# Stacked graph layers on one core: self-loop blocks kept and restored by DMA instead of copies, GpSimd's share of the sums moved to VectorE, and a new rule for spacing the graphs in the planner

## The chip, the cores and the metric

The kernel runs on one NeuronCore of a Trainium2 chip. The metric is the device time of one execution in microseconds (us). Three runs of the kernel before took 2434.01 to 2434.8 us, with a median of 2434.67. The profiled execution, from which all durations below come, took 2439.81 us; its span from the first to the last profiled instruction is 2438.0 us.

## The reference, cut to what matters

There are 32 independent graphs. Each has a feature matrix x of 512 nodes by 256 features and a dense 512 by 512 adjacency matrix whose diagonal is never empty. Four layers follow each other, and each ends in a residual addition and a normalisation over the features. All data is float32.

```python
# layer 0
h = (1 + eps) * x + adj @ x
x = layernorm(x + relu(h @ W1 + b1) @ W2 + b2)            # 256 -> 512 -> 256
# layer 1
h = adj @ (x @ W.T + b)
x = layernorm(x + where(h > 0, h, alpha * h))
# layer 2
h = layer_norm(x, gamma, beta)
x = layernorm(x + (x + relu((adj @ h) @ W_rel + b_rel + h @ W_root)))
# layer 3
h = (eps * x + adj @ x) @ W1 + b1                         # 256 -> 1024
x = layernorm(x + silu(rmsnorm(h, w)) @ W2 + b2)          # 1024 -> 256
```

Layers 0 and 3 multiply by the adjacency with something added to its diagonal: (1 + eps) in layer 0 and eps in layer 3. Layers 1 and 2 use the adjacency as it is.

## The kernel before

**Products.** Most matrix products are done with seven block products instead of eight: `seven` (L552) calls seven products m1 to m7 and adds their results into the four quarters of the output. The price is sums of quarters beforehand: `left_sums` (L570) for the left factor and `right_sums` (L578) for the right one. `left_sums` of the adjacency gives s1 to s4 once per graph, and they serve all four layers. A result leaves PSUM either by a copy (`take`, ScalarE or VectorE) or by an addition on VectorE (`put`, an operand in PSUM).

**The adjacency of a graph** (`class Adjacency`, L599). Four DMA loads of 256 KB bring two halves. `sums` makes s1 to s4. Four pairs of 128 by 128 blocks hold the diagonal: one pair in each of the two loaded halves, one in s1 and one in s3, the last two in one tile (`with_diagonal`). They are copied to a spare tile (`kept`, three copies, one of them for s1 and s3 together, by GpSimd or ScalarE). `with_loops` (L636) writes block plus scaled identity over them, three additions, before layer 0's aggregation and again near the end of layer 2 for layer 3. `restore` (L632) copies the kept blocks back after layer 0's aggregation. `row_sums` (L643) adds up blocks for layer 1's bias.

**Engines.** TensorE does the products and transposes. VectorE does the additions from PSUM, the sums of quarters, and the statistics of the norms. ScalarE does activations, PSUM copies and most of the scaling of the norms. GpSimd takes powers for the inverse square roots (`inv_sqrt`, L484), the additions of a bias row (`plus_row`, L786), and some sums and copies. The queue of SP issues the loads of x and of the adjacency and the stores of the output.

**The order of the work is planned in Python.** Every operation is recorded with the engines that it may run on; where a call names `vector, gpsimd`, either may take it. `Plan.order` (L304) then lists all operations of all graphs: it keeps a clock per engine with the costs of L41 to L71, and at each step takes, among the operations that can start soonest, the one with the lowest rank. The rank of an operation of graph b is b times `period` plus the time at which the graph's own sequence of matmuls needs it, multiplied by `pace`; the last four graphs are set `last` apart instead of `period`. `near` weights operations that feed other engines. `best` (L298) tries every rule of `RULES` (L83) and keeps the order that its clock ends first; for the kernel before, this is period 84, pace 2, last 12, near 2. At most four graphs are in flight (`FLIGHT`, L424). They share 38 tiles of work space and the eight PSUM banks; the last tuple of a pool says how many tiles a graph must leave free, by its distance from the oldest graph in flight: `(0, 2, 2)` for the banks (L437).

The instructions are issued in that order, engine by engine, by one line (L252 for engine instructions, L268 for DMAs), so the profile shows these two lines for nearly everything, and groups are told apart by tiles and shapes. `room` is a work tile, `ps` a PSUM bank, `few` a small tile of statistics.

Of the kernel before, what the change touches and what calls it, by code (L numbers as in the profile page):

```python
# [10 lines left out]
AF = mybir.ActivationFunctionType  # L11
ALU = mybir.AluOpType

P = 128
# [5 lines left out]
def span(ap):  # L20

    n = 1
    for d in ap.shape[1:]:
        n *= d
    return n
# [37 lines left out]
def move_time(kbytes):  # L63
    return kbytes / 370, 2.8


def spread_time():
# [12 lines left out]

RULES = [  # L83
    (period, pace, 12, near)
    for period, pace in ((60, 1), (76, 1), (84, 2))
    for near in (0, 1, 2, 4)
]


class Pool:  # L90
# [91 lines left out]
class Plan:  # L182
# [81 lines left out]
    def move(self, engine, out, src, times, inward=True):  # L264


        def issue():
            getattr(self.nc, engine).dma_start(  # L268
                *(x.place() if isinstance(x, Part) else x for x in (out, src))
            )  # L270

        self.add({engine: (times, issue)}, out if inward else None, [] if inward else [src])

    def needs(self, pace, near):

# [22 lines left out]
    def best(self):  # L298


        rule = min(RULES, key=lambda rule: self.order(*rule)[0])
        return self.order(*rule)[1]
# [84 lines left out]
def tile_gnn_stack(ctx: ExitStack, tc: tile.TileContext, a: dict, out: bass.AP):  # L387
# [26 lines left out]
    B, N, D = a["x"].shape  # L414
# [6 lines left out]
    HC = NC // 2  # L421
    TH = N // 2
    FH = FC3 // 2
# [4 lines left out]
    psum = ctx.enter_context(tc.tile_pool(name="psum", bufs=1, space=bass.MemoryType.PSUM))  # L428
    plan = Plan(nc, FLIGHT)

    def pool(kind, name, n, size, grain, spare):
        return Pool(
            [kind.tile([P, size], F32, tag=f"{name}{i}", name=f"{name}{i}") for i in range(n)],
            grain, spare, kind is psum,
        )

    banks = pool(psum, "ps", 8, N, N, (0, 2, 2))  # L437
    rooms = pool(work, "room", ROOMS, NC * D, P, (0, 4, 6, 8))
    smalls = pool(work, "few", SMALL, 64, 4, (0, 2, 4))

# [1 line left out]
    def vector(method, n, *args, **kw):  # L442
        return "vector", method, vector_time(n), args, kw

    def gpsimd(method, n, *args, **kw):
        return "gpsimd", method, gpsimd_time(n), args, kw

    def scalar(func, n, x, **kw):
        return "scalar", "activation", scalar_time(n), (x,), dict(func=func, **kw)
# [18 lines left out]
    def add(o, x, y, *engines):  # L468
        both("tensor_add", o, x, y, engines or (vector,))

    def sub(o, x, y, *engines):
        both("tensor_sub", o, x, y, engines or (vector,))
# [7 lines left out]

    def stt(o, x, s, y, op0, op1):
        plan.do(o, vector("scalar_tensor_tensor", span(o), x, s, y, op0=op0, op1=op1))

    def inv_sqrt(o, x):  # L484
        n = span(o)
# [5 lines left out]
    def room(*shape):  # L491
        return Part(Room(rooms)).shaped(*shape)
# [76 lines left out]

    def left_sums(left, a21, s):  # L570

        sub(s[2], left["m1"], a21, vector, gpsimd)
        add(s[0], a21, left["m4"], vector, gpsimd)
        sub(s[1], s[0], left["m1"], vector, gpsimd)
        sub(s[3], left["m2"], s[1], vector, gpsimd)
        left.update(m5=s[0], m6=s[1], m7=s[2], m3=s[3])

    def right_sums(b11, b12, b21, b22, t):  # L578

        sub(t[0], b12, b11)  # L580
        sub(t[1], b22, t[0])
        sub(t[2], b22, b12, vector, gpsimd)
        sub(t[3], b21, t[1], vector, gpsimd)
        return dict(m1=b11, m2=b21, m3=b22, m4=t[3], m5=t[0], m6=t[1], m7=t[2])

    def weight_sums(name, a11, a12, a21, a22):
# [12 lines left out]
    class Adjacency:  # L599
# [15 lines left out]
        def sums(self):  # L615
            with_diagonal, others = room(HC, 2, TH), room(2, HC, TH)
            s1, s3 = (with_diagonal[:, :, i, :] for i in range(2))
            s2, s4 = (others[:, i] for i in range(2))
            left_sums(self.left, self.a21, (s1, s2, s3, s4))
            self.loops = [  # L620
                *(self.halves[j].strided(j * TH, (N + P, HC), (1, P)) for j in range(2)),
                with_diagonal.strided(0, (N + P, HC), (TH, 2), (1, P)),
            ]
            kept = room(4 * HC, P)
            self.plain = [
                kept[:, 0:HC], kept[:, HC : 2 * HC],
                kept[:, 2 * HC :].then(lambda v: v.rearrange("p (k s) n -> p k s n", s=2)),
            ]
            for d, o in zip(self.plain, self.loops):
                plan.do(d, gpsimd("tensor_copy", span(o), o), scalar(AF.Copy, span(o), o))  # L630

        def restore(self):  # L632
            for d, o in zip(self.plain, self.loops):
                plan.do(o, gpsimd("tensor_copy", span(o), d), scalar(AF.Copy, span(o), d))

        def with_loops(self, loop):  # L636
            for d, o in zip(self.plain, self.loops):
                wide = loop.unsqueeze(1)
                if len(o.shape) == 4:
                    wide = wide.unsqueeze(1)  # L640
                add(o, d, wide.to_broadcast(list(o.shape)), gpsimd, vector)

        def row_sums(self):  # L643

            rows = room(N)
            s1, a11, a12 = self.left["m5"], self.left["m1"], self.left["m2"]
            add(rows[:, TH:N], s1[:, 0, :], s1[:, 1, :], gpsimd, vector)
            add(rows[:, 0:TH], a11[:, 0, :], a11[:, 1, :], gpsimd, vector)
            for k in range(HC):
                add(rows[:, 0:TH], rows[:, 0:TH], a12[:, k, :], gpsimd, vector)  # L650
            return rows

    def aggregate(x, adjacency):
# [218 lines left out]
    def layer3(x, adjacency, b):  # L872

        aT = aggregate(x, adjacency)
        plus_row(x, b2_3)
        hT, acc = Wide(FC3), room(N)

        def squares(f):
            sq = room(2, N)
            act(sq, hT.pair(f), AF.Square)  # L880
            if f == 0:
                add(acc, sq[:, 0, :], sq[:, 1, :], vector, gpsimd)
            else:
                add(acc, acc, sq[:, 0, :], vector, gpsimd)
                add(acc, acc, sq[:, 1, :], vector, gpsimd)

        dense_feat(aT, A1_3, b1_3, hT, squares)
        few = small(2, NC)
        ve, rstd = few[:, 0, :], few[:, 1, :]
        column_sums(acc, lambda p, sums: ts(ve[p], sums, 1.0 / HID3, RMS_EPS, ALU.mult, ALU.add))  # L890
        inv_sqrt(rstd, ve)
        pr = bank(N)
        for c in range(NC):
            flip(pr[:, c * P : (c + 1) * P], rstd[:, c : c + 1].spread(P, P))
        t1, t2, t4 = (room(FH, TH) for _ in range(3))
        for q in range(0, FH, 2):
            for f in (q, q + 1, FH + q, FH + q + 1):
                mul(hT.chunk(f), hT.chunk(f), pr)
                act(hT.chunk(f), hT.chunk(f), AF.Silu, scale=w_3[:, f : f + 1])
            b11, b12 = (hT.pair(q)[:, :, j * TH : (j + 1) * TH] for j in range(2))  # L900
            b22 = hT.pair(FH + q)[:, :, TH:N]
            t1q, t2q = t1[:, q : q + 2], t2[:, q : q + 2]
            sub(t1q, b12, b11)
            sub(t2q, b22, t1q)
            sub(b12, b22, b12, vector, gpsimd)
            sub(t4[:, q : q + 2], hT.pair(FH + q)[:, :, 0:TH], t2q, vector, gpsimd)
        norm = Norm(x)

        def block(i, j):
            return x[:, j * HC : (j + 1) * HC, i * P : (i + 1) * P]  # L910

        def factor(m, k):
            if m in ("m4", "m5", "m6"):
                return dict(m4=t4, m5=t1, m6=t2)[m][:, k, :]
            f = k if m in ("m1", "m7") else FH + k
            j = 0 if m in ("m1", "m2") else 1
            return hT.chunk(f)[:, j * TH : (j + 1) * TH]

        def product(m, ps, first):
            for k in range(FH):  # L920
                for i in range(HC):
                    mm(
                        ps[:, i, :], factor(m, k)[:, i * P : (i + 1) * P], A2_3[m][:, k, :],
                        first and i == 0 and k == 0, k == FH - 1,
                    )

        def take(ps, i, j):
            add(block(i, j), ps, block(i, j))

        def put(ps, i, j, more):  # L930
            take(ps, i, j)
            if i == 1:
                norm.half(j)

        seven(*(bank(HC, P) for _ in range(3)), product, take, put)
        norm.scales((1.0, LN_EPS))
        y = norm.scaled()
        place = out[b].rearrange("(p c) d -> p c d", c=NC)
        plan.move("sync", place, y, move_time(N * D / 256), inward=False)
# [3 lines left out]
    x = load_x(0)  # L943
# [15 lines left out]
    x = layer0(x, adjacency)  # L959
# [23 lines left out]
    for b in range(1, B):  # L983
        plan.graph = b
        x, adjacency = load_x(b), Adjacency(b)
# [43 lines left out]
```

## Time and profile before

| | |
|---|---|
| device time, median of 3 | 2434.67 us |
| span of the profiled execution | 2438.0 us |
| TensorE clock granted | 0.997 |
| TensorE matmuls | 12808 |
| VectorE busy | 2050.2 us in 5249 instructions |
| ScalarE busy | 1226.0 us in 2490 instructions |
| GpSimd busy | 622.6 us in 677 instructions |
| DMA | 73.89 MB, mean 30 GB/s |

The profile's rows name the line, the engine (PE is TensorE, PEld its weight loads, DVE VectorE, ACT ScalarE, POOL GpSimd, SPq the queue of SP), the operation, and the tiles as output<-inputs. A group's row gives the count, the busy time, the mean of one in ns, and then the idle time of the engine just before its members with what ended it. A row of waits reads: who waited, for whom, total us, how often, the longest. A row of the chain or the timeline begins with the start and the length in us. A float32 matrix product stands in the trace as two matmuls for each one that the kernel writes, except transposes, so 12808 in the trace are 6596 written ones.

### The profile page before, as it was taken

To read this page: it belongs to the slowest core of one execution; us is meant where nothing else is said; L and a number is where in the kernel's file an instruction comes from. 1 tells how busy PE (TensorE), PEld (TensorE's weight loads), DVE (VectorE), ACT (ScalarE), POOL (GpSimd) and SP (SyncE) were. 2 spreads that over 40 slices of the span, in tenths; PEclk is the share of its full clock that TensorE was granted. 3 is DMA by queue.
4 is the path that set the end of the run, shared out by engine and by line. 5 is a ranking of instruction groups with operands and counts; after the bars stand their busy time and mean duration, and the time that the engine had idled before them with its cause. 6 is when DMAs were issued, how large, how long until landed. Compare 5 with 4: busy or idle time off the path is not lost.

```text
span 2438.0 us, 35804 instructions
## 1 busy us (share of the span) xinstructions
PE 2387.9 (98%) x12808; PEld 2117.5 (87%) x12808; DVE 2050.2 (84%) x5249; ACT 1226.0 (50%) x2490; POOL 622.6 (26%) x677
## 2 busy tenths in 40 slices
PE   7999999999999999999999999999999999999998
PEld 6888888888888888888888888888888888888888
DVE  7888888788888889888898788988888888888788
ACT  3454545545455454554554544545445455454464
POOL 2232222222222212232122232223222222222220
PEclk9999999999999999999999999999999999999999
DMA  5011001110011110111101111011110011101000
GB/s 177 1 35 35 10 26 35 36 35 10 27 35 35 35 35 1 35 35 35 35 1 35 35 35 36 1 35 35 35 35 9 28 35 36 35 1 35 1 1 35
DMA packets 34915, 73.89 MB, mean 30 GB/s; under 512 B 6832, under 2 KB 9648, under 8 KB 34736
## 3 DMA queue, kind: packets, MB, share of 16 engines
q1 hardware_dynamic: 30576, 71.05, 8.7%
q8 instruction: 101, 1.65, 0.3%
q10 hardware_dynamic: 4160, 0.54, 0.1%
q14 instruction: 78, 0.64, 0.1%
HBM read 54.80 MB, written 16.78 MB: 29 GB/s over the span
## 4 chain that ended last, share of the span: by engine, by line
PE 71%; DVE 23%; ACT 2%; DMA 2%; issue 1%; SPq 0%; POOL 0%; POOLq 0%; ACTq 0%; DVEq 0%
PE ps L252 71%; DVE room L252 19%; DVE few L252 4%; ACT room L252 2%; DMA room<-in_adj_dram 1%; DMA L_gnn_b<-in_L_gnn_b_dram 0%; SPq L268 0%; DMA room<-in_x_dram 0%; POOL few L252 0%; POOL room L252 0%; ACT L252 0%; POOLq L1025 0%; DVEq L252 0%; ACTq L1025 0%; ACTq L252 0%
## 5 line engine op out<-in xcount | busy, mean ns | idle before, releaser
L252 PE MATMUL ps<-room,room 128*128 128x256 f32 x3584 | 872.5, 382 | 20.7 <-DMA room<-in_x_dram 9.9
L252 PEld LDWEIGHTS ps<-room,room 128*128 128x128 f32 x3584 | 672.5, 191 | 122.3 <-DVE room L252 14.5
L252 DVE TENSOR_TENSOR room<-ps,room 128x256 f32<-128x256 f32 (+1 forms) x1024 | 523.7, 522 | 232.8 <-PE ps L252 194.6
L252 PE MATMUL ps<-L_gnn_W,room 128*128 128x128 f32 (+1 forms) x3584 | 623.0, 322 | 5.3 <-ACT room L252 3.4
L252 ACT ACTIVATE room<-room 128x1024 f32<-128x1024 f32 (+2 forms) x421 | 324.3, 773 | 564.2 <-DVE room L252 293.9
L252 PEld LDWEIGHTS ps<-L_gnn_W,room 128*128 128x128 f32 x3584 | 538.4, 191 | 58.1 <-ACT room L252 8.6
L252 DVE TENSOR_TENSOR room<-room,room 128x512 f32<-128x512 f32 (+1 forms) x825 | 491.4, 603 | 17.1 <-DMA room<-in_adj_dram 7.4
L252 POOL TENSOR_TENSOR few<-few,mhalf 128x4 f32<-128x4 f32 (+1 forms) x160 | 191.1, 1195 | 861.1 <-DVE few L252 860.7
L252 PE MATMUL ps<-room,L_gnn_W 128*128 128x256 f32 x1536 | 395.8, 380 | 2.2 <-DVE room L252 2.1
L252 ACT ACTIVATE room<-ps,L_gnn_b_c 128x256 f32<-128x256 f32 x768 | 314.5, 469 | 154.3 <-PE ps L252 149.8
L252 ACT ACTIVATE room<-ps 128x256 f32<-128x256 f32 (+1 forms) x510 | 200.5, 404 | 334.0 <-PE ps L252 327.9
L252 ACT ACTIVATE room<-room,few 128x256 f32<-128x256 f32 x531 | 282.9, 590 | 80.3 <-DVE few L252 79.6
L252 PEld LDWEIGHTS ps<-room,L_gnn_W 128*128 128x128 f32 x1536 | 286.8, 190 | 41.5 <-DVE room L252 4.8
L252 DVE TENSOR_TENSOR room<-room 128x256 f32<-128x256 f32 (+1 forms) x490 | 240.6, 505 | 82.3 <-DMA room<-in_adj_dram 62.3
L252 PE MATMUL ps<-room,A 128*128 128x256 f32 x1152 | 286.1, 380 | 1.1 <-DVE room L252 0.7
L252 POOL TENSOR_TENSOR room<-room,L_gnn_b 128x256 f32<-128x256 f32 x256 | 191.7, 764 | 324.4 <-PE ps L252 164.4
L252 PEld LDWEIGHTS ps<-room,A 128*128 128x128 f32 x1152 | 213.8, 190 | 30.1 <-ACT room L252 1.8
L252 POOL TENSOR_TENSOR room<-room,room 128x512 f32<-128x512 f32 (+1 forms) x103 | 117.0, 1137 | 380.5 <-ACT room L252 165.8
L252 PE MATMUL ps<-A,room 128*128 128x128 f32 x1536 | 195.8, 277 | 11.3 <-DVE room L252 11.1
L252 ACT ACTIVATE room<-room,L_gnn_rms_weight_c 128x512 f32<-128x512 f32 x256 | 168.8, 714 | 68.5 <-DVE room L252 68.1
L252 PEld LDWEIGHTS ps<-A,room 128*128 128x128 f32 x1536 | 184.3, 192 | 21.0 <-DVE room L252 16.3
L252 DVE BATCH_NORM_STATS2 few<-room 128x6 f32<-128x256 f32 x512 | 198.2, 403 | 0.4
(49 smaller groups left out, 1537.4 us busy)
## 6 DMA issues: line engine op xcount, KB each, us to landing
room<-in_adj_dram SPq DMA_DIRECT2D x128, 256.0 KB, 4.8
room<-in_x_dram SPq DMA_DIRECT2D x32, 512.0 KB, 5.8
out_dram<-room SPq DMA_DIRECT2D x32, 512.0 KB, 3.0
L_gnn_W<-in_L_gnn_W_dram SPq DMA_DIRECT2D x2, 1024.0 KB, 8.2
L_gnn_W<-in_L_gnn_W_dram SPq DMA_DIRECT2D x2, 512.0 KB, 6.8
L_gnn_b<-in_L_gnn_b_dram ACTq DMA_DIRECT2D x3, 128.0 KB, 4.2
L_gnn_W_rel<-in_L_gnn_W_rel_dram SPq DMA_DIRECT2D x1, 256.0 KB, 5.6
L_gnn_W_root<-in_L_gnn_W_root_dram SPq DMA_DIRECT2D x1, 256.0 KB, 5.3
```

The lines of the kernel that those rows point to most:

```text
L252: getattr(getattr(self.nc, engine), method)(put(out), *(put(x) for x in args), **{k: put(x) for k, x in kw.items()})
```

## The change

The three copies that keep the blocks with the diagonal, and the three that restore them, become four DMAs of 128 KB each, issued on the queue of SP (`carry`). The blocks of s1 and s3 are now separate pieces, so `with_loops` makes four additions instead of three. All sums that either VectorE or GpSimd could take are left to VectorE alone: `left_sums`, two of `right_sums`, `with_loops`, `row_sums`, the sums of squares and two sums of layer 3. GpSimd keeps the powers and the bias rows. `move` records the tile that a DMA reads also when it writes a tile. The rules of the planner are two, with a period of 50, a pace of 2, `near` 2 and `last` 12 or 20; `best` keeps `last` 12. A graph other than the oldest leaves one PSUM bank free instead of two.

```diff
-RULES = [
-    (period, pace, 12, near)
-    for period, pace in ((60, 1), (76, 1), (84, 2))
-    for near in (0, 1, 2, 4)
-]
+RULES = [(50, 2, last, 2) for last in (12, 20)]
...
-    banks = pool(psum, "ps", 8, N, N, (0, 2, 2))
+    banks = pool(psum, "ps", 8, N, N, (0, 1, 1))
...
+    def carry(o, x):
+        plan.move("sync", o, x, move_time(P * span(o) / 256))
...
     def left_sums(left, a21, s):
-        sub(s[2], left["m1"], a21, vector, gpsimd)
-        add(s[0], a21, left["m4"], vector, gpsimd)
-        sub(s[1], s[0], left["m1"], vector, gpsimd)
-        sub(s[3], left["m2"], s[1], vector, gpsimd)
+        sub(s[2], left["m1"], a21)
+        add(s[0], a21, left["m4"])
+        sub(s[1], s[0], left["m1"])
+        sub(s[3], left["m2"], s[1])
...
     def right_sums(b11, b12, b21, b22, t):
-        sub(t[2], b22, b12, vector, gpsimd)
-        sub(t[3], b21, t[1], vector, gpsimd)
+        sub(t[2], b22, b12)
+        sub(t[3], b21, t[1])
...
             self.loops = [
                 *(self.halves[j].strided(j * TH, (N + P, HC), (1, P)) for j in range(2)),
-                with_diagonal.strided(0, (N + P, HC), (TH, 2), (1, P)),
+                *(with_diagonal.strided(i * TH, (N + P, HC), (1, P)) for i in range(2)),
             ]
...
             for d, o in zip(self.plain, self.loops):
-                plan.do(d, gpsimd("tensor_copy", span(o), o), scalar(AF.Copy, span(o), o))
+                carry(d, o)
         def restore(self):
             for d, o in zip(self.plain, self.loops):
-                plan.do(o, gpsimd("tensor_copy", span(o), d), scalar(AF.Copy, span(o), d))
+                carry(o, d)
         def with_loops(self, loop):
             for d, o in zip(self.plain, self.loops):
...
-                add(o, d, wide.to_broadcast(list(o.shape)), gpsimd, vector)
+                add(o, d, loop.unsqueeze(1).to_broadcast(list(o.shape)))
```

The same removal of the second engine is made in `row_sums` (four additions), in `squares` (three) and in layer 3's sums of its hidden features (two).

More of the change, by code (lines that the diff above doesn't have):

```diff
@@ L270, in issue @@
             )
-        self.add({engine: (times, issue)}, out if inward else None, [] if inward else [src])
+        self.add(
+            {engine: (times, issue)},
+            out if inward else None, [src] if isinstance(src, Part) else [],
+        )
     def needs(self, pace, near):
@@ L621, in sums @@
                 *(self.halves[j].strided(j * TH, (N + P, HC), (1, P)) for j in range(2)),
-                with_diagonal.strided(0, (N + P, HC), (TH, 2), (1, P)),
+                *(with_diagonal.strided(i * TH, (N + P, HC), (1, P)) for i in range(2)),
             ]
[L624 to L628, printed above, removed]
+            kept = room(4, HC, P)
+            self.plain = [kept[:, i] for i in range(4)]
             for d, o in zip(self.plain, self.loops):
-                plan.do(d, gpsimd("tensor_copy", span(o), o), scalar(AF.Copy, span(o), o))
+                carry(d, o)
         def restore(self):
             for d, o in zip(self.plain, self.loops):
-                plan.do(o, gpsimd("tensor_copy", span(o), d), scalar(AF.Copy, span(o), d))
+                carry(o, d)
         def with_loops(self, loop):
             for d, o in zip(self.plain, self.loops):
-                wide = loop.unsqueeze(1)
-                if len(o.shape) == 4:
-                    wide = wide.unsqueeze(1)
-                add(o, d, wide.to_broadcast(list(o.shape)), gpsimd, vector)
+                add(o, d, loop.unsqueeze(1).to_broadcast(list(o.shape)))
         def row_sums(self):
@@ L646, in row_sums @@
             s1, a11, a12 = self.left["m5"], self.left["m1"], self.left["m2"]
-            add(rows[:, TH:N], s1[:, 0, :], s1[:, 1, :], gpsimd, vector)
-            add(rows[:, 0:TH], a11[:, 0, :], a11[:, 1, :], gpsimd, vector)
+            add(rows[:, TH:N], s1[:, 0, :], s1[:, 1, :])
+            add(rows[:, 0:TH], a11[:, 0, :], a11[:, 1, :])
             for k in range(HC):
-                add(rows[:, 0:TH], rows[:, 0:TH], a12[:, k, :], gpsimd, vector)
+                add(rows[:, 0:TH], rows[:, 0:TH], a12[:, k, :])
             return rows
@@ L881, in squares @@
             if f == 0:
-                add(acc, sq[:, 0, :], sq[:, 1, :], vector, gpsimd)
+                add(acc, sq[:, 0, :], sq[:, 1, :])
             else:
-                add(acc, acc, sq[:, 0, :], vector, gpsimd)
-                add(acc, acc, sq[:, 1, :], vector, gpsimd)
+                add(acc, acc, sq[:, 0, :])
+                add(acc, acc, sq[:, 1, :])
         dense_feat(aT, A1_3, b1_3, hT, squares)
@@ L904, in layer3 @@
             sub(t2q, b22, t1q)
-            sub(b12, b22, b12, vector, gpsimd)
-            sub(t4[:, q : q + 2], hT.pair(FH + q)[:, :, 0:TH], t2q, vector, gpsimd)
+            sub(b12, b22, b12)
+            sub(t4[:, q : q + 2], hT.pair(FH + q)[:, :, 0:TH], t2q)
         norm = Norm(x)
```

## The prediction

> **What bounds the kernel now.** I read the page's engine rows first, then the groups by shape, then matmul starts in the timeline, the waits, and last the chain.
>
> ```profile
> PE 2387.9 (98%) x12808; PEld 2117.5 (87%) x12808; DVE 2050.2 (84%) x5249; ACT 1226.0 (50%) x2490; POOL 622.6 (26%) x677
> ```
>
> TensorE is busy 98% of 2438.0 us. That busy time overstates how near it is to its own pace, so I take the pace from start to start in the timeline:
>
> ```profile
> 697.32 5.34 PE L252 MATMUL ps<-room,room 128*128 128x256 f32 x24
> 702.50 0.59 PE L252 MATMUL ps<-room,L_gnn_W 128*128 128x256 f32 x2
> ...
> 728.01 0.60 PE L252 MATMUL ps<-ident,few 128*128 128x128 f32 x4
> 728.45 0.60 PE L252 MATMUL ps<-L_gnn_W,room 128*128 128x256 f32 x2
> ```
>
> 24 matmuls of 256 columns in 702.50 - 697.32 = 5.18 us are 0.216 us each; 4 of 128 columns in 0.44 us are 0.11 (0.111 over all such pairs). The groups by shape hold 8840 of the first kind and 3968 of the second: 8840 x 0.216 + 3968 x 0.111 = 1909 + 441 = 2350 us, or 73.4 per graph. No part of the change touches them. The first matmul starts at 9.9 us and the last 8.5 us before the end, so 2438 - 2350 - 9.9 - 8.5 = about 69 us are gaps between matmuls: all that can be won or lost cheaply. Read off the matmul starts, 19 of them lie before 300 us (pipeline filling), 45 between 300 and 2050, 5 after. The middle is thus 1.6 us per graph, spread in pieces under 1.5 us.
>
> ```profile
> PE ps L252 <- DVE room L252: 24.7, 47, 1.9
> PEld ps L252 <- DVE room L252: 38.5, 65, 2.3
> PEld ps L252 <- ACT room L252: 20.0, 47, 1.5
> DVE room L252 <- DMA room<-in_adj_dram: 69.7, 20, 5.4
> ACT room L252 <- DMA room<-in_adj_dram: 168.7, 57, 6.2
> ```
>
> TensorE and its weight loads wait for VectorE, then for ScalarE; VectorE and ScalarE in turn stand at the head of their queues for the landing of the next graph's adjacency.
>
> ```profile
> 908.93 5.13 DMA room<-in_adj_dram
> ...
> 1361.03 4.94 DMA room<-in_adj_dram
> ...
> 1810.89 5.59 DMA room<-in_adj_dram
> ```
>
> These pieces of the chain recur each 451 us, six graphs of 75.2 us: there VectorE's wait for a landing reaches the end.
>
> ```profile
> L252 DVE TENSOR_TENSOR room<-room,room 128x512 f32<-128x512 f32 x422 | 318.2, 760 | 11.2 <-DMA room<-in_adj_dram 7.4 <-ACT room L252 1.0
> L252 DVE TENSOR_TENSOR room<-room,ps 128x512 f32<-128x512 f32 x256 | 161.0, 676 | 1.7 <-PE ps L252 1.6
> L252 POOL TENSOR_TENSOR room<-room,room 128x512 f32<-128x512 f32 x58 | 80.0, 1379 | 311.7 <-ACT room L252 165.8 <-DMA room<-in_adj_dram 97.2 <-DVE room L252 29.1
> ...
> 1116.01 1.27 POOL L252 TENSOR_TENSOR room<-room,room 128x512 f32<-128x512 f32 x1 [8.40 <-ACT room L252]
> 1116.29 2.67 DVE L252 TENSOR_TENSOR room<-room,room 128x512 f32<-128x512 f32 x2
> 1117.23 1.18 POOL L252 TENSOR_TENSOR room<-room 128x256 f32<-128x256 f32 x1
> ```
>
> The same sum takes VectorE 676 ns with one operand in PSUM and a mean of 760 (median 681) with both in SBUF. In the timeline two of them last 2.67 us beside GpSimd sums.
>
> **What the skill says.** "SBUF — State Buffer", section "Who interferes with whom": a VectorE instruction with two SBUF inputs and a GpSimd instruction that reads SBUF share one read interface, and the later one blocks. The trace agrees: over all VectorE groups, durations more than 60 ns above their median add up to 89 us, and each of these 178 instructions overlaps a GpSimd sum. "DMA: Bandwidth & Descriptors", section "Anatomy of one DMA", gives about 2.0 us plus bytes at 436 GB/s, so an estimate of 2.3 us for a 128 KB block move; the trace has no SBUF-to-SBUF move, its nearest rows land in 4.8 us (256 KB in) and 3.0 (512 KB out). "Trainium Kernel Development and Optimization", section "Performance Expectations", calls matmul busy time a bad metric, as the 98% against 2350/2438 = 96% shows.
>
> **The change part by part.**
>
> GpSimd's sums go to VectorE. Counting both orders by shape, VectorE gains 76 + 45 sums of 256 elements, 68 of 512, and 164 loop sums of 256 in place of 62 of 512; it loses 35 PSUM copies and 57 norm scalings to ScalarE, since the planner chooses anew. By medians (0.42 and 0.68 us): 121 x 0.42 + 68 x 0.68 + 164 x 0.42 - 62 x 0.68 - 35 x 0.42 - 57 x 0.41 = 50.8 + 46.2 + 68.9 - 42.2 - 14.7 - 23.4 = 86 us. Durations overlap their neighbours: all VectorE durations sum to 2363 us against 2050 busy, 0.06 per instruction, so 200 more instructions give back 12: +74 busy. Against that, the GpSimd sums that go away overlap 67 of the 89 us of blocking; the 22 beside the bias additions (256, which stay) remain. Net +7, VectorE near 2057 us. Bounds: no relief, +74; all relief and tighter packing (0.075 per instruction), about 0. I take +7. GpSimd falls by some 240 us to near 380, waits for nothing that matters, and is free for the powers.
>
> Blocks kept and put back by DMA. ScalarE loses 165 copies (101 x 0.41 + 64 x 0.63 = 82 us) and gains the 57 scalings (0.59) and 35 copies (0.38), 47 us: -35 net; it no longer stands 169 us at adjacency landings with PSUM copies queued behind. SP gains 256 issues of about 0.4 us, 8 per graph, and 33.5 MB beside the 74 MB now, of which SP's 71 take 8.7% of the DMA engines: no load. A keep waits on SP for the adjacency landing; behind it stand keeps, restores and, some 50 to 70 us of matmuls later, the next loads. Restores have 46 us of matmul work before their first reader. The new wait is VectorE's, for a keep before it overwrites the blocks: in the written order there are 17.8 us of matmul work (median, graphs 4 to 28) between a keep and the addition that needs it. Of all 448 such pairs 17 lie under 5 us: graphs 0 and 1 (0.9 to 2.6 us), 4 to 6 (3.3 to 4.3), 29 to 31 (3.5 to 4.8). A landing of 2.3 us is hidden in all but four pairs, of graph 0: about 4 us in sum, less what runs beside it, I take 3, once. Bounds: 0, and with landings of 4.8 us that hold TensorE in every one of the 17 pairs, 29 us.
>
> The order. Planning anew with period 50, pace 2 and one bank fewer held back writes TensorE's rows finer: 5421 rows of like matmuls against 3492. Starts are not a third apart: they come in pairs, 27 and then 120 us of matmul work apart; ends stay 73.4 apart, and a graph stays in flight 215 to 260 us against 270. I count, for each matmul, the matmul work written between it and its nearest producer on another engine. Under 1 us, the tight ones, between 300 and 2000 us: 897 before, 463 after. Before 300: 178, then 118, but 41 and 39 in the first 50 us. After 2000: 122, then 121. Adjacency loads with under 4.8 us before VectorE's first reader: 48 of 100, then 22. VectorE's work per 50 us of matmuls keeps its mean (79 to 82%) but its spread falls from 6.2 to 3.7 points; stretches of 20 us above 95% go from 17 to 11 of 118.
>
> The sum. Middle gaps in proportion to tight matmuls: 45 x 463/897 = 23; I take 21, since blocking and landing waits shrink as well. Start: 19 - 3 (fewer tight ones from 150 us on) + 3 (graph 0's keeps) = 19. Tail 5, ends 9.9 + 8.5. Span 2350 + 21 + 19 + 5 + 18.4 = 2413, which is 25 below 2438.0. The three other runs have a median 3.3 below that span, so 2410, 1.0% faster.
>
> **Rivals.** Gaps in the middle all but vanish (6 us of the 45 left), because unplanned blocking, not tight order, made them: 2413 - 15 - 3 = 2395. For it: 67 us of blocking go. Against: 463 tight matmuls remain, and VectorE still waits 223 us for TensorE, a dependency that no order removes.
>
> No change: the finer order merely moves waits, VectorE's sum and relief cancel, 2435. For it: net VectorE work is +7, and the banks are still eight. Against: the count of tight matmuls.
>
> Slower: VectorE becomes the bound. If blocking stays (bias additions and powers then meet denser sums), it has the full +74 us. The chain
>
> ```profile
> PE 71%; DVE 23%; ACT 2%; DMA 2%; issue 1%; SPq 0%; POOL 0%; POOLq 0%; ACTq 0%; DVEq 0%
> ```
>
> runs through VectorE for 23%, so 0.23 x 74 = 17 us more: 2452. It decides once VectorE's net growth is worth more on the path than the 25 us that the order saves, in the sections of layer 3 where matmuls wait for its products. Against: the 16% idle time of VectorE, and the evener load.
>
> That the change does not do what it says is true of the spacing alone (pairs, not thirds); the 2410 is built on the order as written.
>
> **How the numbers follow.** Gaps halved, 0.67 (2400 to 2424); all but gone, 0.14 (2395); no change, 0.06; slower, 0.13. A measurement of this kernel tells about 0.2% (5 us) from no change. Faster 0.81, same 0.06, slower 0.13. The range 2390 to 2428 covers the first two cases with the keeps' bound; it leaves out the slower case and most of no change.
>
> **What would show it.** Right: groups without GpSimd sums of 512; VectorE's sums of two SBUF operands near 690 ns mean; VectorE busy near 2057; waits of TensorE for VectorE about halved; matmul starts with some 45 us of gaps in all; block moves landing in 2 to 5 us with no large VectorE wait for them. Wrong: a VectorE wait for block moves of tens of us, VectorE over 2110 us busy, or a pace of over 75 us per graph in the middle.

## The result, and the profile after

The changed kernel takes 2393.43 us (median of 4 runs, 2392.34 to 2395.69) against 2434.74 for the kernel before. The ratio is 0.9829 with a 95% interval of 0.9812 to 0.9846: 1.7% faster, 41 us. The forecast was 2410 us in a range of 2390 to 2428. Two single executions that met a lower granted clock stand in no comparison of this document: one of the order alone (0.587, 3970.63 us) and one of the kernel before (0.851, 2749.48 us).

The page's engine rows and the row of the chain, changed kernel:

```profile
PE 2361.3 (99%) x12808; PEld 2113.1 (88%) x12808; DVE 2076.0 (87%) x5449; ACT 1195.2 (50%) x2417; POOL 391.1 (16%) x422
...
PE 95%; DVE 3%; DMA 1%; ACT 1%; issue 0%; POOLq 0%; POOL 0%; ACTq 0%; SPq 0%; DVEq 0%
```

The count of matmuls is the same, and TensorE now carries 95% of the chain instead of 71%. VectorE is busy 26 us longer than before in a span that is 47 us shorter. (The profiled execution of the kernel before, 2439.81 us, lies 5 us above the median of its runs, so spans and gaps taken from profiles differ by a few us more than the times do.) The longest pieces of the chain say where (start, length, what):

```profile
10.51 3.41 DMA room<-room
...
30.11 5.60 DMA room<-room
...
315.74 1818.33 PE ps L248 x9853
```

From 316 to 2134 us the chain does not leave TensorE at all. What is left lies in the first graphs, where two waits for block moves show, and at the end. Some waits of the whole span (who for whom, total, times, longest):

```profile
DVE room L248 <- DMA room<-in_adj_dram: 15.4, 11, 4.4
PEld ps L248 <- DVE room L248: 13.6, 23, 2.8
PEld ps L248 <- ACT room L248: 10.8, 33, 1.1
...
PE ps L248 <- DVE room L248: 6.9, 8, 2.1
DVE room L248 <- DMA room<-room: 6.1, 4, 2.4
```

VectorE's 69.7 us at adjacency landings have become 15.4; TensorE's 24.7 us behind VectorE have become 6.9. Two prices on which the prediction rests are in a group's row and in an issue's row (size, median us to landing):

```profile
L248 DVE TENSOR_TENSOR room<-room,room 128x512 f32<-128x512 f32 x480 | 321.0, 685 | 6.1 <-DMA room<-in_adj_dram 4.6 <-ACT room L248 0.5
...
room<-room SPq DMA_DIRECT2D x256, 128.0 KB, 2.2
```

The sum with both operands in SBUF takes a mean of 685 ns instead of 760, and a block move lands in 2.2 us.

A gap is the time from one matmul's start to the next above its pace (0.216 or 0.111 us). All gaps together were 69 us before and are 20 after. By stage: before 300 us, 19 became 12; from 300 to 2050, called the middle from here on, 45 became 3; after that, 5 stayed 5. The first matmul starts at 10.3 us and the last 9.5 us before the end.

### The profile page after: what moved, and what is told of

Read it like the earlier page. It is cut to its first block, busy times and chain, and to the rows that moved or that the text cites. A ratio compares the mean times of both kernels' runs of the same rounds, so it can differ in the third digit from the quotient of the medians.

```text
span 2390.6 us, 36106 instructions
## 1 busy us (share of the span) xinstructions
PE 2361.3 (99%) x12808; PEld 2113.1 (88%) x12808; DVE 2076.0 (87%) x5449; ACT 1195.2 (50%) x2417; POOL 391.1 (16%) x422
## 4 chain that ended last, share of the span: by engine, by line
PE 95%; DVE 3%; DMA 1%; ACT 1%; issue 0%; POOLq 0%; POOL 0%; ACTq 0%; SPq 0%; DVEq 0%
PE ps L248 95%; DVE room L248 2%; DVE few L248 1%; ACT room L248 1%; DMA room<-room 0%; DMA room<-in_adj_dram 0%; DMA L_gnn_ln_gamma_c<-in_L_gnn_ln_gamma_dram 0%; DMA L_gnn_b_c<-in_L_gnn_b_dram 0%; ACT L248 0%; POOLq L1021 0%; POOL few L248 0%; DVE L_gnn_W L248 0%; DVE A L248 0%; SPq L264 0%; ACTq L1021 0%
## 5 line engine op out<-in xcount | busy, mean ns | idle before, releaser
L248 PE MATMUL ps<-room,room 128*128 128x256 f32 x3584 | 951.8, 381 | 14.0 <-DMA room<-in_x_dram 10.3
L248 PEld LDWEIGHTS ps<-room,room 128*128 128x128 f32 x3584 | 646.7, 191 | 94.2 <-DMA room<-in_x_dram 10.3
L248 PE MATMUL ps<-L_gnn_W,room 128*128 128x128 f32 (+1 forms) x3584 | 667.1, 320 | 2.6 <-ACT room L248 1.5
L248 PEld LDWEIGHTS ps<-L_gnn_W,room 128*128 128x128 f32 x3584 | 581.6, 191 | 61.1 <-ACT room L248 2.4
L248 ACT ACTIVATE room<-room,few 128x256 f32<-128x256 f32 x588 | 311.6, 592 | 328.5 <-DVE few L248 328.4
L248 PE MATMUL ps<-room,L_gnn_W 128*128 128x256 f32 x1536 | 439.5, 379 | 2.9 <-DVE room L248 2.8
L248 PE MATMUL ps<-room,A 128*128 128x256 f32 x1152 | 323.9, 379 | 0.2 <-ACT room L248 0.2
L248 ACT ACTIVATE room<-room 128x1024 f32<-128x1024 f32 (+1 forms) x256 | 238.2, 947 | 31.9 <-DVE room L248 31.2
L248 PEld LDWEIGHTS ps<-A,room 128*128 128x128 f32 x1536 | 226.9, 191 | 16.5
L248 PE MATMUL ps<-A,room 128*128 128x128 f32 x1536 | 233.4, 274 | 0.0
L248 DVE TENSOR_TENSOR room<-room,ps 128x512 f32<-128x512 f32 x256 | 161.9, 681 | 2.6 <-PE ps L248 2.5
```

The source lines that it names most:

```text
L248: getattr(getattr(self.nc, engine), method)(put(out), *(put(x) for x in args), **{k: put(x) for k, x in kw.items()})
```

## The experiments

Three parts can be told apart: the **order** (new rule and banks), the **sums** (VectorE alone) and the **DMA** part. A matmul is called tight, as in the prediction, when under 1 us of matmul work is written between it and its nearest producer on another engine. VectorE's blocking is the time by which its instructions last longer than the median of their shape, where that is over 60 ns. Two theories were set against each other first. Order: the distance that the written order leaves between a producer and its matmul decides, as the prediction had it. Disturbance: VectorE blocked by GpSimd and queues standing at adjacency landings make the gaps, and the order only passes them on.

**The order alone.**

```diff
 (kernel before)
-RULES = [(period, pace, 12, near) for period, pace in ((60, 1), (76, 1), (84, 2)) for near in (0, 1, 2, 4)]
+RULES = [(50, 2, last, 2) for last in (12, 20)]
-    banks = pool(psum, "ps", 8, N, N, (0, 2, 2))
+    banks = pool(psum, "ps", 8, N, N, (0, 1, 1))
```

> The kernel before with the new rules and the banks' (0, 1, 1) alone; GpSimd's sums and the copies stay. Theory Order (the distance that the order leaves between a producer and its matmul decides; between 300 and 2000 us of matmul work it has 554 tight matmuls against 897 before and 463 after): most of the gain is here, 2395 to 2405 us. Theory Disturbance (gaps come from VectorE being blocked by GpSimd's sums and from queues standing at adjacency landings, and the order only passes them on): the sums and copies still disturb, 2418 us or more.

2428.41 us, ratio 0.9972 (0.9961 to 0.9984): 7 us of the 41. The same kernel once more gives the profile:

> The new rules and banks alone once more, for a profile. The median so far is 2428. If the order still leaves the gaps, they are spread over the whole middle at VectorE's and ScalarE's waits for adjacency landings and beside GpSimd's sums (Disturbance); if the order is good and only ends are bad, the middle has under 10 us of gaps and the rest lies before 300 us and after 2000.

2428.73 us in a single run. The middle still has 40 us of gaps, with 554 tight matmuls against 897, so a count reduced by four tenths won a tenth of the gaps there. But ScalarE's waits for adjacency landings fell from 168.7 us to 18.4 and VectorE's from 69.7 to 18.1:

```profile
DVE few L248 <- POOL few L248: 40.1, 29, 1.7
...
ACT room L248 <- DMA room<-in_adj_dram: 18.4, 9, 5.7
DVE room L248 <- DMA room<-in_adj_dram: 18.1, 17, 4.6
```

So landings are not what makes the gaps of this order. Neither theory in this form stands; GpSimd beside VectorE was left. Its blocking is 100 us in this run, and 163 us when it is measured from each shape's 5th percentile instead of its median: in one shape of 128 instructions the median itself was 1.21 us against 0.67 free. VectorE also waits 40 us for GpSimd's powers here (5 us in the kernel before).

**The sums alone, and the DMA part alone**, both with the rule held at (84, 2, 12, 2), because the planner would choose another one: run from the kernel's file with all twelve rules of before, its clock ends the sums alone at 2460.5 us under this rule, the worst of the twelve, and at 2418.6 us under the best.

```diff
 (kernel before, rule fixed)
-        sub(s[2], left["m1"], a21, vector, gpsimd)
+        sub(s[2], left["m1"], a21)
 ... and so for every shared sum
```

> The kernel before with all shared sums on VectorE alone; rule fixed at the one of before (84, 2, 12, 2), banks and copies as before. Order: 993 tight matmuls in the middle, about as before, so 2432 to 2440 us. Disturbance: two thirds of the blocking go, so 2412 to 2425 us. If VectorE is the bound, its 74 us more make it 2445 us or more.

2499.65 us, ratio 1.0264 (1.0249 to 1.0279). Slower by 65 us: the prediction's slower rival, which the changed kernel does not show, is real under this rule. That it is so under the other old rules is not shown. VectorE is blocked for only 31 us in this run, yet the middle has 91 us of gaps and TensorE waits twice as long for VectorE:

```profile
DVE room L248 <- PE ps L248: 276.3, 290, 5.2
...
PE ps L248 <- DVE room L248: 49.4, 49, 2.4
...
PE ps L248 <- ACT room L248: 21.3, 35, 2.2
```

A part of these gaps is TensorE's clock. The row of a stretch (window, its length, TensorE busy, granted clock, DMA share and GB/s) reads 1.00 ahead of three stops and 0.50 behind them:

```profile
1272.00:1280.00 8.00, 8.00 (x39) 1.00 0.01 2
1286.90:1293.70 6.80, 5.86 (x16) 0.50 0.00 0
```

Six such stretches, 27 us long in all, hold 13 of the 91 us; each begins within 5 us of a stop of over 1 us. The changed kernel has none in the middle. So some long stops cost more here than their own length.

```diff
 (kernel before, rule fixed)
-                plan.do(d, gpsimd("tensor_copy", span(o), o), scalar(AF.Copy, span(o), o))
+                carry(d, o)
 ... and the same in restore; four separate blocks and additions instead of three
```

> The kernel before with the blocks kept and put back by DMA alone; rule fixed at (84, 2, 12, 2), GpSimd still shares the sums. Order: 942 tight matmuls in the middle, so 2430 to 2438 us. Disturbance: ScalarE no longer stands at adjacency landings, VectorE and GpSimd still do, so 2420 to 2430 us.

2448.85 us, ratio 1.0060 (1.0043 to 1.0077): slower by 14 us. The middle keeps its gaps (44 us); the losses that the profiles show, 9 us, are at the start (24 against 19) and the end (9 against 5).

**The old order, sums moved in place.** The list is that of the kernel before, operation for operation; only the engine of the sums changes when they are issued.

```diff
 (kernel before, in Plan.do's issue)
+            if engine == "gpsimd" and method in ("tensor_add", "tensor_sub") and len(ways) > 1:
+                engine = "vector"
```

> The order of the kernel before, operation for operation, but every addition or subtraction that the planner gave to GpSimd though VectorE could take it is issued on VectorE, at its place in the list. Order: tight matmuls as before, so 2430 to 2440 us. Disturbance: blocking by these sums is gone, so 2410 to 2422 us. VectorE as the bound: 2445 us or more, since it has the extra work at places where the plan counted on GpSimd.

2445.32 us, ratio 1.0041 (1.0026 to 1.0056). Blocking falls from 89 us to 31 and the middle's gaps go from 45 to 48. This run takes the blocking away and adds work to VectorE at the same places, so it doesn't show what the blocking alone is worth.

The second set undoes one part each in the changed kernel. The theories were now Blocking (GpSimd's sums make the gaps of the finer order) and Landing (ScalarE's wait for adjacency does).

```diff
 (changed kernel)
-        sub(s[2], left["m1"], a21)
+        sub(s[2], left["m1"], a21, vector, gpsimd)
 ... and so for every sum that was shared
```

> The changed kernel with GpSimd allowed to share the sums again, so new order and DMA keeps without the sums' part. Theory Blocking (in the finer order it is GpSimd's sums beside VectorE's that make the gaps): 2412 to 2425 us. Theory Landing (it is ScalarE standing at adjacency landings with PSUM copies behind it, which DMA keeps end): 2392 to 2402 us.

2451.33 us, ratio 1.0063 (1.0048 to 1.0078): the whole gain and more is lost. It has 462 tight matmuls in the middle and 55 us of gaps there; the changed kernel has 463 and 3. The count of tight matmuls is thereby refuted as a measure. The gaps are two stops in nearly every graph, of about 1.3 and 0.6 to 0.8 us. The chain of this kernel through one of the longer ones begins with a stretch of VectorE:

```profile
1052.69 4.08 DVE room L248 x5
...
1063.07 0.61 ACT room L248
1063.67 0.04 issue
1063.72 0.48 PE ps L248
```

The timeline of the same stretch (in square brackets: idle time before, and what ended it) shows what happens in it:

```profile
1054.57 1.65 POOL L248 TENSOR_TENSOR room<-room,room 128x512 f32<-128x512 f32 x1 [3.36 <-DVE room L248]
...
1055.02 1.75 DVE L248 TENSOR_TENSOR room<-room,room 128x512 f32<-128x512 f32 x1
...
1063.07 1.58 ACT L248 ACTIVATE room<-room,few 128x256 f32<-128x256 f32 x3 [9.95 <-DVE few L248]
...
1063.72 0.70 PE L248 MATMUL ps<-room,room 128*128 128x256 f32 x2 [1.20 <-ACT room L248]
```

VectorE works ten microseconds almost without a pause towards a norm of layer 1, ScalarE waits 9.95 us for its statistics, and TensorE for ScalarE. One sum blocked by GpSimd takes 1.75 us instead of 0.68, so 1.07 more, and TensorE's stop is of that order (1.37 us beyond its pace).

```diff
 (changed kernel)
-                carry(d, o)
+                plan.do(d, gpsimd("tensor_copy", span(o), o), scalar(AF.Copy, span(o), o))
 ... and the same in restore
```

> The changed kernel with the blocks kept and put back by ScalarE or GpSimd copies, so new order and sums on VectorE without the DMA part. Blocking: 2392 to 2402 us. Landing: 2412 to 2425 us. If each is half of it, both this and the one with the sums given back lie between 2402 and 2415 us.

2387.04 us (2386.52 to 2387.27), ratio 0.9798 (0.9782 to 0.9814): no loss, rather 6 us less than the changed kernel; no run of one overlaps a run of the other, but the intervals of the two ratios just touch. Landing falls. The copies here are of the four separate blocks of the changed kernel. The 6 us lie before 300 us, where this kernel has 6.5 us of gaps against 12.1.

```diff
 (changed kernel)
-RULES = [(50, 2, last, 2) for last in (12, 20)]
+RULES = [(84, 2, 12, 2)]
-    banks = pool(psum, "ps", 8, N, N, (0, 1, 1))
+    banks = pool(psum, "ps", 8, N, N, (0, 2, 2))
```

> The sums on VectorE and the keeps by DMA, with the rule of the kernel before (84, 2, 12, 2) and its banks (0, 2, 2). Alone, these parts took the kernel before to 2500 and 2449 us. If the old spacing cannot carry the fuller VectorE: 2445 us or more. If the two parts help each other whatever the order: under 2425 us.

2461.43 us, ratio 1.0101 (1.0086 to 1.0116). With or without DMA, sums on VectorE lose under the old rule (84, 2, 12, 2). Of the 58 us of gaps in the middle, 11 lie in stretches at a granted clock of 0.5.

The third set asks what in "order with sums" it is.

```diff
 (changed kernel with the sums given back)
+            if engine == "gpsimd" and method in ("tensor_add", "tensor_sub") and len(ways) > 1:
+                engine = "vector"
```

> The order of the changed kernel with sums given back (2451 us), operation for operation, but the 381 additions and subtractions that it gave to GpSimd are issued on VectorE at their places. Theory GpSimd (their running beside VectorE makes the gaps: VectorE was blocked for 170 us in that run): back to 2385 to 2405 us, though VectorE has more work than the plan counted on. Theory Plan (the order written for a sharing GpSimd is itself the worse one): 2440 us or more.

2438.77 us, ratio 1.0015 (1.0008 to 1.0022): 13 us less than with GpSimd executing them, but 45 us above the changed kernel. Theory GpSimd fails in this form, and the time lies 1 us under what Theory Plan asked for; here too VectorE carries work that the plan gave to GpSimd. At the same stop the sum that was blocked now takes its normal time, and another VectorE sum stands in the stretch; TensorE's stop shrinks from 1.37 to 0.79 us beyond its pace:

```profile
1047.40 1.28 DVE L250 TENSOR_TENSOR room<-room,room 128x512 f32<-128x512 f32 x2
...
1050.40 0.68 DVE L250 TENSOR_TENSOR room<-room,room 128x512 f32<-128x512 f32 x1
...
1057.99 1.58 ACT L250 ACTIVATE room<-room,few 128x256 f32<-128x256 f32 x3 [10.08 <-DVE few L250]
...
1058.64 0.70 PE L250 MATMUL ps<-room,room 128*128 128x256 f32 x2 [0.62 <-ACT room L250]
```

```diff
 (changed kernel)
-    banks = pool(psum, "ps", 8, N, N, (0, 1, 1))
+    banks = pool(psum, "ps", 8, N, N, (0, 2, 2))
```

> The changed kernel with two PSUM banks held back for the younger graphs as before, (0, 2, 2); the planner then takes last 20. If the third free bank carries the finer order, the gaps return in part: 2405 us or more. If the spacing of the graphs does it alone: 2390 to 2403 us (438 tight matmuls in the middle against 463).

2400.45 us, ratio 0.9856 (0.9840 to 0.9873). The middle has 0.4 us of gaps; the loss of 7 us lies after 2050 (15.5 us of gaps against 5.2), where the planner now sets the last graphs 20 apart. The bank that is no longer held back is not what empties the middle.

```diff
 (changed kernel)
-            add(x[:, c, :], x[:, c, :], r, gpsimd)
+            add(x[:, c, :], x[:, c, :], r)
```

> The changed kernel with the additions of the bias rows on VectorE too, so GpSimd keeps only the powers. The 43 us of blocking that are left go, and VectorE gains 256 x 0.34 = about 86 us, net +43, to some 2119 us busy. Theory GpSimd: the middle has no gaps left to win, so 2385 to 2397 us. Rival, VectorE as the bound: it gets to 89% of the span and 2405 us or more.

2387.77 us, ratio 0.9804 (0.9789 to 0.9819). No VectorE instruction is blocked any more, and VectorE is fuller still:

```profile
PE 2358.6 (99%) x12808; PEld 2116.2 (89%) x12808; DVE 2103.5 (88%) x5678; ACT 1210.2 (51%) x2444; POOL 198.1 (8%) x166
```

256 more additions on VectorE cost nothing where the plan knows of them. VectorE as a bound by sheer load is excluded up to this level.

```diff
 (changed kernel with the copies back)
-RULES = [(50, 2, last, 2) for last in (12, 20)]
+RULES = [(50, 2, 16, 1)]
```

> The kernel with the copies back (2387 us) under the rule (50, 2, 16, 1): near 1 and last 16. All gaps there were 14 us, 6 before 100 us and 5 after 2100, so at most some 10 us are to be had: 2380 to 2390 us. It tells whether a version under 2387 is near; over 2393 would say that near 2 matters in the middle.

2382.24 us, ratio 0.9784 (0.9769 to 0.9798): 11 us under the changed kernel, with an interval that lies below that one's, and no gap over 0.03 us between 300 and 2050. Its waits and chain:

```profile
ACT room L248 <- DMA room<-in_adj_dram: 65.8, 44, 2.8
```

```profile
183.07 1970.71 PE ps L248 x10720
```

ScalarE stands at adjacency landings 44 times, and TensorE never stops for 1971 us. So these waits at the head of a queue cost TensorE nothing here.

**What the planner's own clock says.** The planner allows for blocking: `port` in `Plan.order` never lets a GpSimd sum overlap, on the planner's clock, a VectorE instruction that has no input in PSUM (the norms' statistics apart). Where such a pair blocks on the chip, it ran at other times than planned. On this clock the old order has stops of TensorE in the middle, 16 us for the kernel before and 74 with the sums on VectorE; the new order has none, with shared sums as little as without.

How much of the measured gaps is written in the order, and how much does blocking add? For an estimate the written lists can be replayed with the planner's costs: each operation starts as soon as its engine, its inputs and its tiles allow, and VectorE and GpSimd may overlap. A second replay lengthens each VectorE instruction by its blocking in the trace (here from the 5th percentile of its shape). Neither replay has measured landings or the lower clock in it.

**The cases side by side** (us; gaps and blocking are worked out from the starts and durations in each trace; "tight" counts matmuls between 300 and 2000 us of matmul work; the last two columns are the estimates of the middle's gaps, without and with blocking):

| order | sums | blocks | time | gaps in the middle | VectorE blocked | tight | replay | with blocking |
|---|---|---|---|---|---|---|---|---|
| old | shared (before) | copies | 2434.7 | 45 | 89 | 897 | 11 | 42 |
| old | shared, moved in place | copies | 2445.3 | 48 | 31 | 897 | 47 | 52 |
| old | VectorE | copies | 2499.7 | 91 | 31 | 993 | 62 | 67 |
| old | shared | DMA | 2448.9 | 44 | 75 | 942 | 24 | 45 |
| old | VectorE | DMA | 2461.4 | 58 | 27 | 878 | 39 | 45 |
| new | shared | copies | 2428.4 | 40 | 100 (163) | 554 | 0 | 26 |
| new | shared | DMA | 2451.3 | 55 | 170 | 462 | 0 | 38 |
| new | shared, moved in place | DMA | 2438.8 | 37 | 49 | 462 | 23 | 24 |
| new | VectorE (changed kernel) | DMA | 2393.4 | 3 | 43 | 463 | 0 | 1 |
| new | VectorE | copies | 2387.0 | 3 | 49 | 519 | 0 | 1 |

The middle is empty exactly where the new rule and the sums on VectorE come together. With copies, the sums cost 65 us in the old order and save 41 in the new one; the order saves 7 us with shared sums and 113 with VectorE alone.

The estimates give a reason for this. The stops have two sources. The old order writes some of them, and more when VectorE has all the sums; blocking by GpSimd's sums makes the rest. The new order writes none but leaves the blocking, and even more of it, as long as the sums are shared. Only the two parts together remove both. Moving the sums in place removes the blocking but puts work into VectorE's queue that the plan had not counted there, and that alone gives 47 and 23 us. The replay falls short by 14 to 17 us in the new order with shared sums and by 13 where they are moved in place; of the 24 and 13 us that it lacks in the two old orders with sums on VectorE, 13 and 11 are the lower clock.

## Why the prediction was right, and where its size was off

The floor held: 2350 us of matmul pace, and the span after is 2350 + 10.3 + 9.5 + 20, within 1 us. Direction, range and the place of the gain were right. The forecast saving was 25 us against 41 measured. That the time fell into the range is in part luck. The forecast puts the gain down to the order, but the order alone saves 7 us, where its proportion would have taken 17 us from the middle (45 x 554/897 = 28).

The mis-sized term is the middle gaps, "45 x 463/897 = 23; I take 21", which came out at 3. The step that fails is the proportion: kernels with 462 and 463 tight matmuls had 55 and 3 us of gaps. The count looks only at the last step before a matmul, while at the stop shown above a whole VectorE stretch runs late, the ten microseconds before 1063.72. The rival with the gaps all but gone gave 2395 and lies nearest. Its reason, unplanned blocking, is by the replays the larger source before the change, 31 of the 42 us that they account for; the 463 tight matmuls that were held against it leave no gaps. It is not the whole reason: without any blocking the sums on VectorE would still have some 62 us of stops in the old order.

One sum of the prediction is off: 45 us in 1750 us are 1.9 us per graph of 75.2 us, not 1.6. Nothing else rests on it.

VectorE's sum: 2057 forecast, 2076 measured. The relief was over-sized: with VectorE denser, the 256 bias additions blocked 111 of its instructions for 43 us instead of 55 for 22. It cost little: with these additions on VectorE the middle's 3 us become 0.4.

The landing of a block move was priced rightly, 2.2 us against 2.3. That estimate came from the Trainium skill, "DMA: Bandwidth & Descriptors", section "Anatomy of one DMA", which states its fit for DMAs that GpSimd issues; here it held on the queue of SP. The waits for block moves were larger than the 3 us taken, though inside the bounds: VectorE waits 6.1 us in 4 pieces, and two landings of 3.41 and 5.60 us stand in the chain. All of them lie in the first graphs, as forecast. In the middle the DMA part is not needed; copies do as well.

The Trainium skill, "SBUF — State Buffer", section "Who interferes with whom", lets a VectorE instruction with two SBUF inputs contend with any GpSimd instruction that reads SBUF. The blocked sums of 1.75 us against 0.68 agree with it. GpSimd's powers do not: they read SBUF too, but once GpSimd kept only them, 287 VectorE additions of two SBUF operands overlapped a power and none lasted over 0.02 us longer than the median of its shape.

The slower rival named a real mechanism and the wrong condition. It was to decide by VectorE's load; what decided was where the load stands. VectorE is busy 2083 us in the kernel at 2500 us, and 2104 us in the one at 2388.

What stays open: what else holds up the new order with shared sums, where the replays account for 26 of 40 and 38 of 55 us; how the sums on VectorE would do under the best of the old rules, which was not run; and why the clock was lowered behind some long stops and not behind others.

## What to carry to other kernels

In a kernel planned against one saturated engine, a part's worth is not its own: test parts in pairs before judging one, since here each of three parts alone gave between 7 us saved and 65 lost, and two together saved 48. Ask the planner first which stops it has written itself, and then what the chip adds to them. Give work to the engine whose times the plan knows, even if it is the fuller one, and look at the whole stretch ahead of a stop rather than at the last wait. A transfer that replaces a short copy is worth its price only where the copy stood in the way.

## What the runs showed of the hardware that was not expected

Blocking between VectorE and GpSimd reaches VectorE's smallest instructions too: in the changed kernel 50 statistics operations of 0.16 us took 0.2 to 0.5 us longer beside a bias addition. Beside a power of GpSimd no VectorE instruction was blocked. A block move of 128 KB between work tiles held the queue of SP 0.594 us per issue (median), against 0.43 for the adjacency loads of 256 KB. With the sums alone, TensorE's granted clock fell to 0.5 for 3.4 or 6.8 us behind some of its long stops.
